# The start of an attention and FFN layer, its weight looks and its late flag on one Trainium2 core

## The chip, the core and the metric

The kernel runs on one core of a Trainium2 chip. The engines are TensorE (PE in the profile; PEld is its weight load), VectorE (DVE), ScalarE (ACT), GpSimd (POOL) and SyncE (SP, which only issues DMAs here). ACT and POOL also issue DMAs from their own queues; such rows carry a q (ACTq, SPq). The metric is the device time of one execution in microseconds (us), the median of several runs. A profile shows one execution.

## The reference

The inputs are x of 2 batches by 2048 rows by 256 features, four 256x256 attention weights, and a feed-forward net with 1024 hidden features whose weights hold only -1, 0 and 1, with a scale per output.

```
xn  = layernorm(x)
q, k, v = xn @ Wq, xn @ Wk, xn @ Wv
attn = softmax(causal(q @ k.T) / 16)          # one head of 256
a   = (attn @ v) @ Wo
h   = silu((xn @ w1.T) * s1) * ((xn @ w2.T) * s2)
h   = gelu((h @ h1.T) * sh1);  h = gelu((h @ h2.T) * sh2)     # exact gelu
out = x + a + (h @ w3.T) * s3
```

Everything is float32 and the outputs must be accurate to float32 inputs, so the kernel splits most operands into a high part that TensorE takes (fp32r) and a low part, the rest: a product is then two or three matmuls.

## The kernel before

**Stages.** The rows are cut into eight blocks of 512 (`TB`), four to a batch (`NB`). The attention of both batches comes first, then the feed-forward net. One branch lies between them: `ffn_ternary` for weights that are -1, 0 and 1, `ffn` for any others. The branch reads `flag`, which the attention stage works out while it runs.

**Start.** `load_x` fetches a block of x in two halves on SP. Wq and Wk come on ACT's queue. `weights_product` folds Wq and Wk into one matrix `wqk`, and later Wv and Wo into `wvo`; each half of a product has its own PSUM bank and copies (L260 to L267). `keys(n)` normalizes a block (`start_keys`: statistics L275 and L276 on VectorE, the root on ScalarE L280, four scalings on GpSimd L320), transposes it on TensorE (L346), and `hi_lo` (L251, L252) splits it on ScalarE and VectorE; the result also goes to DRAM (`xT_d`, L348) for the feed-forward stage. `queries` (L357), `score` (L401, mask L407, eviction with maximum L410) and `values` (L373) follow. Until x is there TensorE runs `WARM` matmuls on zeros (L247).

**Attention.** For each tile of 128 rows, `score` leaves its results in `s`, ScalarE takes the exponential (L422), and the tile is transposed: by blocks of 32 on VectorE (`turn_blocks`, L292) and two DMAs through DRAM (`d<-b` L297, `e<-d` L304), or for short tiles on TensorE (L465). Its high part pT is copied by ScalarE (L460, L251), the low part by GpSimd (L461) or VectorE, and `weigh` multiplies with the values (L479, L484; eviction L499 and L500). The second batch's x is normalized on GpSimd in the middle of this (L320), and its keys are split on ScalarE and GpSimd (L338, L339). Four PSUM banks `ps_0` to `ps_3` are used in turn by all products but `weigh` and the transposes.

**Looks.** Beside the attention the kernel looks through all feed-forward weights for a value that is not -1, 0 or 1. `items` lists the work and `beside(cost)` releases one step whenever enough matmul columns have gone by. `item_low` fetches a piece, rounds it on GpSimd (L134), masks the low bits on VectorE (L558) and adds them up on ScalarE (L560). `item_factors` takes two pieces of h1, forms four sums of their quarters on VectorE (`sum_up`, L153) into the buffer `xh0`, stores them (L581) and then runs `odd` on each piece: ScalarE takes the absolute value in place (L565), VectorE compares `(t != 0) != t` and adds up (L567). Its last step, `copy_factors`, copies three quarters of h1 from DRAM to DRAM on ACT's queue (L584, L586). `item_signs` runs `odd` on a piece of h2. The pieces arrive in two buffers `stg` by DMAs on ACT's queue (`fetched_weights`, L622); a fetch waits until the look that last used its buffer is done. `tc.issue_after(mark)` keeps an instruction behind a marked one of the main stream on its engine.

**The flag.** When the last look has been released, the loop at the end of the attention stage takes the maximum of all sums (L742), multiplies it into one number (L744) and copies it to `flag` (L745).

**Order.** Programs are written in stages, but the framework orders instructions per engine by a planned timeline when it builds the kernel; each engine then runs its list in order, and waits on semaphores. So a step may stand on its engine well before or after its place in the text.

**Feed-forward.** `ffn_ternary` runs on pairs of blocks: gated products (L172), then seven half-size products in place of eight for h1 and h2 (L850, with sums of weight quarters, the `factors`, read from DRAM), then w3 (L1011). The change does not touch it.

Of the kernel before, what the change touches and what calls it, by code (L numbers as in the profile page):

```python
# [31 lines left out]
TURN_KEYS = [8, 10, 12, 14]  # L32
LOOKS_FROM = 3
LEAD = 2
WARM = 14

STEPS = [("A11", "B11"), ("S1", "T1"), ("S2", "T2"), ("S4", "B22"), ("S3", "T3"), ("A12", "B21"), ("A22", "T4")]

SLOTS = {"h1": range(7), "h2": (0, 4, 1, 3, 2, 5, 6)}
LOW_BITS = 0xFFF


# [20 lines left out]
def attn_ffn_kernel(  # L65
# [57 lines left out]

    HB = H // 2
    HK = HC // 2
    factors = {k: dram.tile([P, len(STEPS), HK, HB], F32, name=f"factors_{k}") for k in ("h1", "h2")}


# [60 lines left out]
    with ExitStack() as actx:  # L189
# [19 lines left out]

        def bank():  # L210
            return in_turn("ps", ps_tiles)

        def load_x(n):
            t = xp.tile([P, NT, D], F32, tag="x", name=f"x_{n}")
            for h in range(2):
                src = x[n // NB, ds((n % NB) * TB + h * 2 * P, 2 * P), :]
                nc.sync.dma_start(out=t[:, ts(h, 2), :], in_=src.rearrange("(t p) d -> p t d", p=P))
            return t

        xs[NB - 1] = load_x(NB - 1)  # L220
        raw = {}
        for name, src in (("q", wqT), ("k", wkT)):
            raw[name] = stgp.tile([P, DC, D], F32, tag="stg", name=f"raw_{name}")
            nc.scalar.dma_start(out=raw[name], in_=src)
        nc.scalar.preload_act_table(AF.Sqrt)
        for n in range(NB - 2, -1, -1):
            xs[n] = load_x(n)

        ident = cp.tile([P, P], F32, name="ident")
        make_identity(nc, ident)  # L230
# [9 lines left out]
        nc.gpsimd.memset(ones, 1.0)  # L240


        idle = sp.tile([P, S], F32, tag="s", name="idle")[:, : TB // 2].bitcast(BF16)
        nc.vector.memset(idle, 0.0)
        ps_idle = bank()
        for _ in range(WARM):
            nc.tensor.matmul(out=ps_idle, lhsT=idle[:, :P], rhs=idle, start=True, stop=True)  # L247

        def hi_lo(hi, lo, src):

            nc.scalar.copy(hi, src)  # L251
            nc.vector.tensor_tensor(lo, src, hi.bitcast(F32), ALU.subtract)  # L252

        def weights_product(name, aT, b, factor):

            r = cp.tile([P, DC, 2, D], F32R, name=name)
            for c in range(DC):
                ps = bank()
                for d in range(DC):
                    nc.tensor.matmul(  # L260
                        out=ps[:, :D], lhsT=aT[:, d, ts(c, P)], rhs=b[:, d, :],
                        start=(d == 0), stop=(d == DC - 1),
                    )
                f = rp.tile([P, NT + 1, D], F32, tag="r", name=f"wf_{name}_{c}")[:, 0, :]
                nc.scalar.mul(f, ps[:, :D], factor)
                nc.vector.tensor_copy(r[:, c, 0, :], f)
                nc.vector.tensor_tensor(  # L267
                    r[:, c, 1, :], f, r[:, c, 0, :].bitcast(F32), ALU.subtract
                )
            return r  # L270

        def stats(xt, mv, n):
            for t in range(NT):
# [38 lines left out]
        def start_keys(n):  # L312
            xt = xs.pop(n)
            if n not in rstds:
                mv = cp.tile([P, NT, 2], F32, name=f"mv_{n}")
                stats(xt, mv, n)
                rstds[n] = root(mv, NT, str(n))
            rstd, off = rstds[n]
            for t in range(NT):
                nc.gpsimd.tensor_scalar(  # L320
                    xt[:, t, :], xt[:, t, :], rstd[:, t : t + 1], off[:, t : t + 1],
                    ALU.mult, ALU.add,
                )
            return xt
# [5 lines left out]
        def keys(n):  # L330
            ks[n] = kp.tile([P, DC, 2, TB], F32R, tag="k", name=f"k_{n}")
            if n in turned_keys:
                xT = turned_keys.pop(n).rearrange("p (t c) i q -> p c t i q", c=DC)
                for c in range(DC):
                    hi, lo = (
                        ks[n][:, c, a, :].rearrange("p (t i q) -> p t i q", t=NT, q=Q) for a in range(2)
                    )
                    nc.scalar.copy(hi, xT[:, c])  # L338
                    nc.gpsimd.tensor_tensor(lo, xT[:, c], hi.bitcast(F32), ALU.subtract)  # L339
# [8 lines left out]
            nc.sync.dma_start(out=xT_d[n], in_=ks[n].bitcast(F32).rearrange("p c h t -> p (c h t)"))  # L348

        def queries(n, m):  # L350
            if m == 0:
                qs[n] = in_turn("q", q_tiles)
            pp = bank()
            k = 0
            for c in range(DC):
                for a, b in ((0, 0), (0, 1), (1, 0)):
                    nc.tensor.matmul(  # L357
                        out=pp, lhsT=wqk[:, c, a, ts(m, P)], rhs=ks[n][:, c, b, :],
                        start=(k == 0), stop=(k == 3 * DC - 1),
                    )  # L360
                    k += 1
            hi_lo(qs[n][:, m, 0, :], qs[n][:, m, 1, :], pp)
# [18 lines left out]


        state, attn = {}, {}
        marks = {}

        def score(n, t, m, order):
            first = n - n % NB
# [8 lines left out]
            at = (m - first) * TB  # L396
            ps = bank()
            k = 0
            for c in range(DC):
                for a, b in ((0, 0), (0, 1), (1, 0)):  # L400
# [45 lines left out]
        def turn(n, t, m):  # L446
# [20 lines left out]
                )  # L467
            hi_lo(pT[:, 0, :w], pT[:, 1, :w], pt[:, :w])

        def weigh(n, t, m):  # L470
            first = n - n % NB
            st = state[n, t]
            if m == first:
# [87 lines left out]

        def odd(t):

            with tc.issue_after(marks["ACT"]):
                nc.scalar.activation(t, t, AF.Abs)  # L565
            with tc.issue_after(marks["DVE"]):
                nc.vector.scalar_tensor_tensor(  # L567
                    t, t, 0.0, t, ALU.not_equal, ALU.not_equal, accum_out=seen()
                )
# [24 lines left out]
        def item_factors(src, f, c):  # L594
# [12 lines left out]
        for src, dst in ((w1, w1_sb), (w2, w2_sb)):  # L607
            for c in range(src.shape[1]):
                item_low(src[:, c, :], dst[:, c, :])
# [92 lines left out]
        def before(j):  # L702
            if 3 <= j < 3 + NB:
                n = NB + j - 3
                x1 = xs[n] = load_x(n)
# [11 lines left out]
        now = 0  # L717
        until = -1
        j = -1
        checked = False  # L720
        while until < len(tiles) - 1:
            j += 1
            while until + 1 <= j - AHEAD:
# [12 lines left out]
            now += sum(cost for cost, _ in a + b)  # L736
            scored.append(now)
            merged(a, b, beside)
            if not looks and not checked:
                checked = True  # L740
                most = small.tile([P, 1], F32, tag="most", name="most")
                nc.vector.reduce_max(most, low_bits[:, : looked[0]], axis=AX.X)  # L742
                pf = bank()
                nc.tensor.matmul(out=pf[:1, :1], lhsT=most, rhs=ones, start=True, stop=True)  # L744
                nc.vector.tensor_copy(flag, pf[:1, :1])  # L745

        assert checked
# [474 lines left out]
```

## Time and profile before

| | before |
|---|---|
| median of 3 runs (lowest to highest) | 871.73 us (871.02 to 874.87) |
| the profiled execution's own time | 872.82 us |
| its span, first to last instruction | 871.1 us |
| busy TensorE, VectorE, ScalarE, GpSimd | 852.2, 620.4, 504.9, 296.4 us |
| feed-forward stage (from the branch on) | from about 287 us |
| TensorE's mean granted clock | 0.990 |

The span is cut into 40 slices in the page; a digit is a busy share in tenths, and PEclk is the clock that TensorE was granted, in tenths of full speed. In a timeline row the columns are start, length (of all the merged instructions), engine, line, operation, output and inputs, shape and count; in brackets stands how long the engine was idle before it and whom it waited for. In a row of the waits the numbers are the total, the count and the longest wait. A window row gives its length, then busy time and count for PE, PEld, DVE, ACT and POOL, then the granted clock, the busy share of the DMA engines and GB/s.

### The profile page before, as it was taken

What the parts mean: (1) busy time and instruction counts of PE and PEld (TensorE: products, weight loads), DVE (VectorE), ACT (ScalarE), POOL (GpSimd) and SP (SyncE); (2) the same over time, 40 slices, a digit from 0 to 9 for tenths busy, and PEclk for the clock granted to TensorE, in tenths of its full rate; (3) what the DMA queues carried; (4) which work ended last, traced back from release to release, by engine and by line L of the source; (5) the groups of instructions that cost most, each with busy time, mean ns of one, the idle gap of its engine ahead of it and who ended that gap; (6) DMA issues with size and microseconds to landing.
All of it is one profiled execution on the core that took longest, in us unless ns stands there. A gap on an engine that the chain in (4) does not pass through costs nothing.

```text
span 871.1 us, 12205 instructions
## 1 busy us (share of the span) xinstructions
PE 852.2 (98%) x4280; PEld 720.1 (83%) x4280; DVE 620.4 (71%) x1065; ACT 504.9 (58%) x881; POOL 296.4 (34%) x242
## 2 busy tenths in 40 slices
PE   8999799999999999999999999999999999999997
PEld 5988688888887878888988888988888898888887
DVE  5687664784764699996596596569468648848764
ACT  2556556764666456677256586536557635657670
POOL 4034857433544476550142050025024003502300
PEclk8999989999999999999999999999999999999999
DMA  9876499766792898854334434432444431144411
GB/s 307 331 250 212 152 348 292 265 214 194 251 343 62 340 400 309 312 192 146 111 109 150 144 144 146 148 121 103 146 145 145 146 136 58 50 144 145 145 49 53
DMA packets 62679, 162.53 MB, mean 187 GB/s; under 512 B 6544, under 2 KB 36368, under 8 KB 53264
## 3 DMA queue, kind: packets, MB, share of 16 engines
q1 hardware_dynamic: 56048, 141.73, 46.6%
q10 hardware_dynamic: 5472, 15.73, 5.3%
q0 software_dynamic: 1088, 4.19, 1.2%
q8 instruction: 36, 0.59, 0.3%
q14 instruction: 35, 0.29, 0.1%
HBM read 120.21 MB, written 47.71 MB: 193 GB/s over the span
## 4 chain that ended last, share of the span: by engine, by line
PE 75%; DMA 9%; DVE 6%; issue 3%; ACT 3%; POOL 2%; SPq 2%; ACTq 0%; POOLq 0%; DVEq 0%
PE ps_own L850 23%; PE ps L850 23%; PE ps L172 5%; PE ps_own L172 5%; PE ps L401 5%; DMA e<-d 4%; PE ps_own L1011 4%; PE ps L1011 4%; POOL pT L461 2%; DMA d<-b 2%; PE ps L373 2%; PE po L479 2%; PE ps L357 2%; SPq L304 1%; DMA d_x<-b 1%
## 5 line engine op out<-in xcount | busy, mean ns | idle before, releaser
L401 PE MATMUL ps<-k,q 128*128 128x512 f32 (+3 forms) x480 | 109.6, 366 | 0.0
L461 POOL TENSOR_TENSOR pT<-e,pT 128x512 fp32r<-128x512 f32 (+3 forms) x60 | 74.8, 1264 | 72.5 <-ACT pT L460 55.6
L401 PEld LDWEIGHTS ps<-k,q 128*128 128x128 f32 x480 | 82.0, 189 | 12.2
L479 PE MATMUL po<-v,pT 128*128 128x512 f32 x272 | 79.6, 406 | 6.6 <-ACT pT L460 6.5
L982 POOL TENSOR_TENSOR rt<-rt,xt 128x1024 f32<-128x1024 f32 x8 | 21.5, 2706 | 165.2 <-issue 114.7
L871 ACT ACTIVATE k_h_u<-k_h_u,h_s_sb 128x512 f32<-128x512 f32 x64 | 45.9, 722 | 38.1 <-DVE k_h_u L870 37.5
L830 POOL TENSOR_TENSOR k_h_u<-k_h_p,k_h_u 128x512 f32<-128x512 f32 x16 | 23.2, 1452 | 123.1 <-ACT q L185 106.3
L479 PEld LDWEIGHTS po<-v,pT 128*128 128x128 f32 x272 | 48.1, 193 | 14.5 <-ACT pT L460 7.2
L410 DVE TENSOR_SCALAR_CACHE_REDUCE s<-ps 128x512 f32<-128x512 f32 (+3 forms) x80 | 47.1, 600 | 12.1 <-PE ps L407 8.1
L422 ACT ACTIVATE s<-s,low 128x1024 f32<-128x1024 f32 (+7 forms) x48 | 43.0, 898 | 21.7 <-DVE low L416 21.7
L292 DVE STREAM_TRANSPOSE b<-s 128x1024 f32<-128x1024 f32 (+3 forms) x30 | 33.5, 1128 | 22.8 <-ACT s L422 20.5
L460 ACT CAST pT<-e 128x512 fp32r<-128x512 f32 (+3 forms) x60 | 32.4, 574 | 27.4 <-DMA e<-d 25.0
L484 PEld LDWEIGHTS po<-v,pT 128*128 128x128 f32 x272 | 42.0, 190 | 6.5 <-POOL pT L461 1.7
L484 PE MATMUL po<-v,pT 128*128 128x256 f32 x272 | 46.9, 286 | 0.2 <-POOL pT L461 0.2
L186 DVE TENSOR_TENSOR q<-k_h_u,q 128x512 fp32r<-128x512 f32 x32 | 45.9, 1462 | 0.0
L889 POOL TENSOR_TENSOR k_h_p<-f_h_B,k_h_p 128x512 f32<-128x512 f32 x16 | 34.4, 2175 | 21.2 <-DVE h_h_T L186 21.2
L500 POOL TENSOR_TENSOR r<-r 128x256 f32<-128x256 f32 x32 | 24.4, 765 | 49.7 <-ACT r L499 49.7
L830 POOL TENSOR_TENSOR f_w_B<-f_w_B,f_w_B 128x512 f32<-128x512 f32 x16 | 26.0, 1646 | 33.0 <-DVE f_w_B L181 33.0
L172 PE MATMUL ps<-xh,w_sb 128*128 128x512 f32 x144 | 35.9, 392 | 0.0
L870 DVE TENSOR_TENSOR k_h_u<-ps_own,k_h_u 128x512 f32<-128x512 f32 x32 | 21.7, 686 | 17.8 <-PE ps_own L850 17.8
L871 ACT ACTIVATE k_h_p<-k_h_p,h_s_sb 128x512 f32<-128x512 f32 x32 | 22.8, 722 | 18.6 <-DVE k_h_p L870 18.6
L850 PE MATMUL ps<-q,w_h_A 128*128 128x512 f32 x128 | 31.2, 393 | 1.5 <-DVE f_w_B L181 1.5
(176 smaller groups left out, 2201.3 us busy)
## 6 DMA issues: line engine op xcount, KB each, us to landing
w_h_S<-factors_h SPq DMA_DIRECT2D x32, 1024.0 KB, 4.7
w_h_A<-factors_h SPq DMA_DIRECT2D x24, 1024.0 KB, 4.7
d<-b SPq DMA_DIRECT2D x18, 512.0 KB, 3.5
e<-d SPq DMA_DIRECT2D x72, 128.0 KB, 3.6
xT_d<-k SPq DMA_DIRECT2D x8, 1024.0 KB, 7.3
stg<-in_ffn_h_w ACTq DMA_DIRECT2D x16, 512.0 KB, 5.6
x<-in_attn_x SPq DMA_DIRECT2D x16, 256.0 KB, 5.9
factors_h<-xh SPq DMA_DIRECT2D x4, 1024.0 KB, 4.8
```

What stands on the lines that cost most here:

```text
L172: nc.tensor.matmul(out=p, lhsT=w[:, c, ts(o, P)], rhs=xh[:, c, a, :], start=(c == 0 and a == 0), stop=(c == DC - 1 and a == 1),)
L186: nc.vector.tensor_tensor(r[:, 1, :], f, r[:, 0, :].bitcast(F32), ALU.subtract)
L401: nc.tensor.matmul(out=ps[:, :w], lhsT=qs[n][:, c, a, ts(t, P)], rhs=ks[m][:, c, b, :w], start=(k == 0), stop=(m < n and k == 3 * DC - 1),)
L410: marks["DVE"] = nc.vector.tensor_scalar(st["s"][:, ds(at, w)], ps[:, :w], 1.0, None, ALU.mult, ALU.max, accum_out=st["tops"][:, m - first ...
L422: marks["ACT"] = nc.scalar.activation(st["s"][:, at], st["s"][:, at], AF.Exp, bias=low, accum_out=st["sums"][:, u // UK : u // UK + 1],).ins
L461: nc.gpsimd.tensor_tensor(lo, src, hi.bitcast(F32), ALU.subtract)
L479: nc.tensor.matmul(out=st["po"], lhsT=pT[:, 0, ts(j, P)], rhs=vs[m][:, j, :, :], start=(m == first and j == 0), stop=False,)
L484: marks["PE"] = nc.tensor.matmul(out=st["po"][:, 0, :], lhsT=pT[:, 1, ts(j, P)], rhs=vs[m][:, j, 0, :], start=False, stop=(m == n and j == ...
L830: nc.gpsimd.tensor_tensor(B["B12"][i], B["B22"][i], B["B12"][i], ALU.subtract)
L850: nc.tensor.matmul(out=out[o], lhsT=w[:, c, ts(o, P)], rhs=sets[right][c][:, a, :], start=(start and c == 0 and a == 0), stop=(c == HK - 1 ...
L871: nc.scalar.activation(C[k][o], r[o] if r else banks[o], AF.Gelu, scale=s[:, at : at + 1])
L1011: nc.tensor.matmul(out=ys[t][:, :D], lhsT=h[c][:, a, ts(t, P)], rhs=w3_sb[:, c, :], start=(c == 0 and a == 0), stop=(c == HC - 1 and a == 1),)
```

## The change

The first block of x comes by SP and ACT's queue, one half each; Wq and Wv come behind it on SP, Wk and Wo on ACT's queue, with Wv and Wo in the buffer `b_1`. Both weight products are multiplied at the start, each into one bank, and copied in one piece later. Two of the four rows of the first xn are scaled by ScalarE. The statistics of the next blocks are kept behind `wqk`'s low part. The warm-up is 26 matmuls of half the width, with six more in the text behind the first keys. Queries and scores take the high parts first. h1's DRAM copies leave the looks and follow the four `xT_d` writes on SP. `odd` takes the absolute value by masking the sign bit on VectorE. The fetches of looked-at weights stay behind the last exponential. The flag is worked out in `judge`, called ahead of the last `weigh`.

```diff
-WARM = 14
+WARM = 26
+WARM_KEYS = 6
...
+MAGNITUDE = 0x7FFFFFFF
...
-        xs[NB - 1] = load_x(NB - 1)
-        raw = {}
-        for name, src in (("q", wqT), ("k", wkT)):
-            raw[name] = stgp.tile([P, DC, D], F32, tag="stg", name=f"raw_{name}")
-            nc.scalar.dma_start(out=raw[name], in_=src)
+        xs[NB - 1] = load_x(NB - 1, (nc.sync, nc.scalar))
+        raw = {name: stgp.tile([P, DC, D], F32, tag="stg", name=f"raw_{name}") for name in "qk"}
+        for i, name in enumerate("vo"):
+            raw[name] = b_tiles[1][:, i, :].rearrange("p (c d) -> p c d", c=DC)
+        for name, src, queue in (
+            ("q", wqT, nc.sync), ("k", wkT, nc.scalar), ("v", wvT, nc.sync), ("o", wo, nc.scalar)
+        ):
+            queue.dma_start(out=raw[name], in_=src)
...
+        def keep_warm(k):
+            for _ in range(k):
+                nc.tensor.matmul(
+                    out=ps_idle[:, : TB // 2], lhsT=idle[:, :P], rhs=idle[:, : TB // 2], start=True, stop=True
+                )
+
+        keep_warm(WARM)
...
             r = cp.tile([P, DC, 2, D], F32R, name=name)
+            ps = bank().rearrange("p (c d) -> p c d", c=DC)
             for c in range(DC):
-                ps = bank()
...
+            def copied():
+                f = rp.tile([P, NT + 1, D], F32, tag="r", name=f"wf_{name}")[:, :DC, :]
+                nc.scalar.mul(f, ps, factor)
+                nc.vector.tensor_copy(r[:, :, 0, :], f)
+                marks["lo"] = nc.vector.tensor_tensor(
+                    r[:, :, 1, :], f, r[:, :, 0, :].bitcast(F32), ALU.subtract
+                ).ins
+
+            return r, copied
...
+                with ExitStack() as behind:
+                    if n < NB - 1:
+                        behind.enter_context(tc.issue_after(first_lo))
+                    stats(xt, mv, n)
...
+                if n == NB - 1 and t % 2:
+                    nc.scalar.activation(
+                        xt[:, t, :], xt[:, t, :], AF.Identity,
+                        scale=rstd[:, t : t + 1], bias=off[:, t : t + 1],
+                    )
+                    continue
...
-            for c in range(DC):
-                for a, b in ((0, 0), (0, 1), (1, 0)):
+            for a, b in ((0, 0), (1, 0), (0, 1)):
+                for c in range(DC):
...
+        def judge():
+
+            assert not looks
+            most = small.tile([P, 1], F32, tag="most", name="most")
+            nc.vector.reduce_max(most, low_bits[:, : looked[0]], axis=AX.X)
+            with tc.issue_after(marks["PE"]):
+                pf = bank()
+                nc.tensor.matmul(out=pf[:1, :1], lhsT=most, rhs=ones, start=True, stop=True)
+            nc.vector.tensor_copy(flag, pf[:1, :1])
+
         def weigh(n, t, m):
+            if (n, t, m) == (N - 1, NT - 1, N - 1):
+                judge()
...
         def odd(t):
 
-            with tc.issue_after(marks["ACT"]):
-                nc.scalar.activation(t, t, AF.Abs)
             with tc.issue_after(marks["DVE"]):
+                nc.vector.tensor_scalar(t.bitcast(U32), t.bitcast(U32), MAGNITUDE, None, ALU.bitwise_and)
                 nc.vector.scalar_tensor_tensor(
...
         def copy_factors(src, f, c):
-            nc.scalar.dma_start(out=f[:, 0, c, :], in_=src[:, c, :HB])
-            for i in range(2):
-                nc.scalar.dma_start(out=f[:, 5 + i, c, :], in_=src[:, c + HK, ts(i, HB)])
+            with tc.issue_after(marks["SP"]):
+                nc.sync.dma_start(out=f[:, 0, c, :], in_=src[:, c, :HB])
+                for i in range(2):
+                    nc.sync.dma_start(out=f[:, 5 + i, c, :], in_=src[:, c + HK, ts(i, HB)])
...
-                (3000, lambda t: copy_factors(src, f, c)),
...
-                nc.scalar.dma_start(out=t, in_=src)
+                with tc.issue_after(marks["ACT"]):
+                    nc.scalar.dma_start(out=t, in_=src)
...
-        wqk = weights_product("wqk", raw["q"], raw["k"], scale)
-        for name, src in (("v", wvT), ("o", wo)):
-            raw[name] = stgp.tile([P, DC, D], F32, tag="stg", name=f"raw_{name}")
-            nc.scalar.dma_start(out=raw[name], in_=src)
+        wqk, wqk_copied = weights_product("wqk", raw["q"], raw["k"], scale)
+        wvo, wvo_copied = weights_product("wvo", raw["v"], raw["o"], 1.0)
         keys(NB - 1)
+        wqk_copied()
+        first_lo = marks["lo"]
+        keep_warm(WARM_KEYS)
         queries(NB - 1, 0)
         queries(NB - 1, 1)
         order = list(range(NB - 1, -1, -1))
         score(NB - 1, NT - 1, NB - 1, order)
-        wvo = weights_product("wvo", raw["v"], raw["o"], 1.0)
+        with tc.issue_after(marks["hi"]), tc.issue_after(marks["lo"]):
+            wvo_copied()
+        copy_factors(h1, factors["h1"], 0)
         for n in order[1:]:
             keys(n)
+            copy_factors(h1, factors["h1"], NB - 1 - n)
...
-            if not looks and not checked:
-                checked = True
-                most = small.tile([P, 1], F32, tag="most", name="most")
...
```

More of the change, by code (lines that the diff above doesn't have):

```diff
@@ L125, in attn_ffn_kernel @@
     HK = HC // 2
+    assert HK == 2 * DC == NB
     factors = {k: dram.tile([P, len(STEPS), HK, HB], F32, name=f"factors_{k}") for k in ("h1", "h2")}
@@ L211, in bank, with load_x @@
             return in_turn("ps", ps_tiles)
-        def load_x(n):
+        marks = {}
+        def load_x(n, queues):
             t = xp.tile([P, NT, D], F32, tag="x", name=f"x_{n}")
-            for h in range(2):
+            for h, queue in enumerate(queues):
                 src = x[n // NB, ds((n % NB) * TB + h * 2 * P, 2 * P), :]
-                nc.sync.dma_start(out=t[:, ts(h, 2), :], in_=src.rearrange("(t p) d -> p t d", p=P))
+                queue.dma_start(out=t[:, ts(h, 2), :], in_=src.rearrange("(t p) d -> p t d", p=P))
             return t
-        xs[NB - 1] = load_x(NB - 1)
-        raw = {}
-        for name, src in (("q", wqT), ("k", wkT)):
-            raw[name] = stgp.tile([P, DC, D], F32, tag="stg", name=f"raw_{name}")
-            nc.scalar.dma_start(out=raw[name], in_=src)
+        xs[NB - 1] = load_x(NB - 1, (nc.sync, nc.scalar))
[6 more added lines that the diff above has]
+            queue.dma_start(out=raw[name], in_=src)
         nc.scalar.preload_act_table(AF.Sqrt)
         for n in range(NB - 2, -1, -1):
-            xs[n] = load_x(n)
+            xs[n] = load_x(n, (nc.sync, nc.sync))
         ident = cp.tile([P, P], F32, name="ident")
@@ L240, in attn_ffn_kernel @@
         nc.gpsimd.memset(ones, 1.0)
-        idle = sp.tile([P, S], F32, tag="s", name="idle")[:, : TB // 2].bitcast(BF16)
+        idle = sp.tile([P, S], F32, tag="s", name="idle")[:, : TB // 4].bitcast(BF16)
         nc.vector.memset(idle, 0.0)
         ps_idle = bank()
-        for _ in range(WARM):
-            nc.tensor.matmul(out=ps_idle, lhsT=idle[:, :P], rhs=idle, start=True, stop=True)
+        def keep_warm(k):
[4 more added lines that the diff above has]
+        keep_warm(WARM)
         def hi_lo(hi, lo, src):
-            nc.scalar.copy(hi, src)
-            nc.vector.tensor_tensor(lo, src, hi.bitcast(F32), ALU.subtract)
+            marks["hi"] = nc.scalar.copy(hi, src).ins
+            marks["lo"] = nc.vector.tensor_tensor(lo, src, hi.bitcast(F32), ALU.subtract).ins
         def weights_product(name, aT, b, factor):
             r = cp.tile([P, DC, 2, D], F32R, name=name)
+            ps = bank().rearrange("p (c d) -> p c d", c=DC)
             for c in range(DC):
-                ps = bank()
                 for d in range(DC):
                     nc.tensor.matmul(
-                        out=ps[:, :D], lhsT=aT[:, d, ts(c, P)], rhs=b[:, d, :],
+                        out=ps[:, c, :], lhsT=aT[:, d, ts(c, P)], rhs=b[:, d, :],
                         start=(d == 0), stop=(d == DC - 1),
                     )
[L264 to L270, printed above, removed]
+            def copied():
[6 more added lines that the diff above has]
+            return r, copied
         def stats(xt, mv, n):
@@ L315, in start_keys @@
                 mv = cp.tile([P, NT, 2], F32, name=f"mv_{n}")
-                stats(xt, mv, n)
+                with ExitStack() as behind:
+                    if n < NB - 1:
+                        behind.enter_context(tc.issue_after(first_lo))
+                    stats(xt, mv, n)
                 rstds[n] = root(mv, NT, str(n))
@@ L347, in keys @@
                 hi_lo(ks[n][:, c, 0, :], ks[n][:, c, 1, :], pt)
-            nc.sync.dma_start(out=xT_d[n], in_=ks[n].bitcast(F32).rearrange("p c h t -> p (c h t)"))
+            marks["SP"] = nc.sync.dma_start(out=xT_d[n], in_=ks[n].bitcast(F32).rearrange("p c h t -> p (c h t)")).ins
         def queries(n, m):
@@ L383, in attn_ffn_kernel @@
         state, attn = {}, {}
-        marks = {}
         def score(n, t, m, order):
@@ L398, in score @@
             k = 0
-            for c in range(DC):
-                for a, b in ((0, 0), (0, 1), (1, 0)):
+            for a, b in ((0, 0), (0, 1), (1, 0)):
+                for c in range(DC):
                     nc.tensor.matmul(
@@ L605, in item_factors @@
             items.append(([src[:, c, :], src[:, c + HK, :]], steps))
-        for src, dst in ((w1, w1_sb), (w2, w2_sb)):
-            for c in range(src.shape[1]):
-                item_low(src[:, c, :], dst[:, c, :])
+        for c in range(HK):
+            src, dst = ((w1, w1_sb), (w2, w2_sb))[c // DC]
+            item_low(src[:, c % DC, :], dst[:, c % DC, :])
         w3_at = list(range(0, HC, SC // D))
@@ L704, in before @@
                 n = NB + j - 3
-                x1 = xs[n] = load_x(n)
+                x1 = xs[n] = load_x(n, (nc.sync, nc.sync))
                 with tc.issue_after(marks["DVE"]):
@@ L719, in attn_ffn_kernel @@
         j = -1
-        checked = False
         while until < len(tiles) - 1:
@@ L738, in attn_ffn_kernel @@
             merged(a, b, beside)
-            if not looks and not checked:
-                checked = True
-                most = small.tile([P, 1], F32, tag="most", name="most")
[L742 to L747, printed above, removed]
         last_quarter = [bank(), bank()]
```

## The prediction, made before the changed kernel ran

> **What bounds the kernel now.** I read the page's busy shares and slices first, then the waits of TensorE (PE), then windows and the timeline around the two places where PE is not both busy and at full clock.
>
> ```profile
> PE 852.2 (98%) x4280; PEld 720.1 (83%) x4280; DVE 620.4 (71%) x1065; ACT 504.9 (58%) x881; POOL 296.4 (34%) x242
> PE   8999799999999999999999999999999999999997
> PEclk8999989999999999999999999999999999999999
> ```
>
> PE is busy for 98% of the span, so 18.9 us is all the idle time there is, about 6.3 of it the tail after the last matmul, which the change does not touch. The fifth slice of PE (7) and the two slices with a clock of 8 are where something can be won.
>
> ```profile
> 8.00:11.00 3.00, 1.78 (x9) 0.80 (x8) 2.38 (x10) 1.00 (x3) 2.17 (x4) 0.99 1.08 387
> 11.00:17.00 6.00, 5.21 (x11) 3.64 (x12) 4.74 (x21) 1.40 (x5) 2.42 (x5) 0.50 0.89 287
> ```
>
> Windows: PE's busy time is the second number, the granted clock the one before the DMA share. From 8 to 11 us PE is busy for 1.78 of 3 us, and then the clock is 0.50 until 17. The first queries (L357) run there at half speed.
>
> ```profile
> PE po L479 <- ACT pT L460: 6.5, 4, 4.8
> PE ps L850 <- DVE f_w_B L181: 1.5, 2, 1.2
> PE ps L357 <- DVE v L252: 0.5, 1, 0.5
> ```
>
> Waits of PE: one single wait, 4.8 us for ScalarE's copy of pT, is a quarter of all PE idle time. The timeline shows its history:
>
> ```profile
> 102.14 4.38 DVE L153 TENSOR_TENSOR xh<-stg,stg 128x512 fp32r<-128x512 f32 x1
> 103.49 2.47 POOL L339 TENSOR_TENSOR k<-x,k 128x512 fp32r<-128x512 f32 x2
> 107.28 1.06 ACT L565 ACTIVATE stg<-stg 128x1024 f32<-128x1024 f32 x1 [3.80 <-DVE xh L153]
> 108.24 0.60 ACT L460 CAST pT<-e 128x512 fp32r<-128x512 f32 x1
> 108.36 1.23 DVE L567 SCALAR_TENSOR_TENSOR stg<-stg 128x1024 f32<-128x1024 f32 x1 [0.40 <-ACT stg L565]
> 108.89 2.08 PE L479 MATMUL po<-v,pT 128*128 128x512 f32 x4 [4.75 <-ACT pT L460]
> ...
> 110.68 1.18 DVE L567 SCALAR_TENSOR_TENSOR stg<-stg 128x1024 f32<-128x1024 f32 x1
> 111.79 0.68 DVE L410 TENSOR_SCALAR_CACHE_REDUCE s<-ps 128x512 f32<-128x512 f32 x1
> ...
> 113.45 2.96 PE L357 MATMUL ps<-k,wqk 128*128 128x512 f32 x12
> ```
>
> VectorE's (DVE's) sum L153, 0.69 in its other places, stands 4.38 beside GpSimd's (POOL's) run of two-input operations, which ends at 105.96. ScalarE (ACT) waits 3.80 for it with the look L565, and the pT copies stand behind that look. PE waits 4.75, and its clock falls:
>
> ```profile
> 104.00:109.00 5.00, 0.25 (x2) 0.11 (x1) 4.57 (x5) 1.72 (x3) 2.05 (x3) 0.75 0.09 35
> 109.00:114.00 5.00, 5.00 (x15) 3.86 (x16) 4.69 (x12) 2.47 (x5) 4.69 (x3) 0.56 1.02 321
> ```
>
> A mean clock of 0.56 over 5 us costs about 2.2 us more. So the place is worth about 7 us.
>
> **The start.** I work in the profiled run's time: span 871.1, its own time 872.8, which is 1.1 above the median of 871.7. In the order of the built kernel PE runs 32 warm-up matmuls of half the width, then the products of Wq Wk and of Wv Wo, then the first transposes, the queries, the first scores. The six extra warm-up matmuls meant for later stand in front with the rest. In the trace seven of the 14 old ones take 0.427 each, to 4.2 us, the others 0.22; so 32 halves end at 4.2 + 18 x 0.116 (a 128x256 of L484) = 6.3. The product took 1.97 for eight, so Wq Wk ends at 8.3 and Wv Wo at 10.2; eight transposes at 0.19 end at 11.8. Before, they ended at 10.73. So although xn is ready sooner (both halves of x at 4.4 where the second came at 6.02; two rows on POOL, 2 x 0.54, beside two on ACT, done at 8.3 and not 10.24), that gain is covered by the product moved in front. Four weight loads are 1 MB beside 0.5 MB of x; at the measured 370 to 400 GB/s they land by about 7, ahead of their use.
>
> From there: ACT's copies of k end at 12.6; eight queries need only k's high half and run to 14; DVE has four 0.36 statistics of the next x ahead of the first low half and three between the two, so the low halves come at 12.8 and 14.7, and the queries end at 15.3 (before 17.65). The next x is normalized by 18.2, q's low halves come at 18.7, the scores with their mask end at 19.1, the first values wait for wvo's low half until 20.35. Before, PE had reached the same count of matmuls at 22.47. Gain 2.1, if the clock stays at 1.00; bounds 0 (a second stretch at 0.50) and 4.4 (all of the queries' 2.35 and the product's 2.05).
>
> h1's twelve copies of 256 KB leave ACT's queue and stand on SP behind the four writes of xT, ahead of the first d<-b. By 40 us the queues have moved about 13 MB in both kernels, at up to 400 GB/s; the two early stg loads are gone from there, and I find the backlog done at 37 where d is issued at 40.5. Cost nothing; if it collides, the first pT has 1.3 us of slack at PE (ready 52.4, used 53.72), so at most 1.5. Hi-first order of queries and scores costs nothing in a stage where PE is busy throughout.
>
> **The looks.** Each of 16 `odd` loses 1.05 on ACT and gains an in-place bitwise_and on DVE:
>
> ```profile
> L558 DVE TENSOR_SCALAR stg<-stg x6: 687/1070/1759, 69.9 to 264.3; 128x1024 uint32<-128x1024 uint32 x6
> ```
>
> 0.69 with POOL quiet, 1.07 in the median, 1.76 beside POOL's L461. Now the place at 104, in before's time. The orders of DVE and POOL up to it are the same, so I expect the 4.38 again and the three sums done at 107.97. ACT no longer waits: pT comes at 104.8 and PE goes on after 0.9, then waits for POOL's low half (about 108), and comes to the queries at 109.4. These need a PSUM bank whose eviction (L410) stands on DVE behind two bitwise_ands, two L567 and a block transpose: 107.97 + 2 x 0.69 to 1.07 + 1.23 + 1.24 + 1.18 + 0.68 = 113.7 to 114.4. PE started L357 at 113.45. So the wait does not go, it changes its owner: from "ACT pT" to "DVE s". PE starts the queries 0.6 later, and cold after 4.6 us of idleness, where before it had warmed up by then; the price of that is the 2.2 above plus its first cold matmuls, I take 2.3. Together +2.9; bounds -4.0 (sum not blocked: below) and +5.4 (POOL's two L461, ready sooner now, go first and DVE loses 2.5 more). ACT's weight loads (L622) still wait on its queue for the look that frees their buffer, with pT copies behind them.
>
> The Trainium skill, in "SBUF — State Buffer", section "SBUF: two separate sides", says that DVE and GpSimd share one pair of ports as an exclusive lock, and that the loser is blocked for the whole instruction. By that rule every one of the 16 new operations can lose a POOL instruction of 1.27, which speaks against the change; the 1.76 of L558 agrees, its 0.69 elsewhere shows that it is not the usual price.
>
> Elsewhere PE's six waits between 120 and 280 make 2.75, 1.78 of it for ACT's pT, 0.80 for DVE. The first should shrink, the second grow by one pair of 0.69: I take 0, bounds -2.7 and +4.2 (three more pairs of looks, each 1.4 later).
>
> The flag: reduce_max, one small matmul (0.19) and the copy come before the last eight po matmuls; 1.4 us of these and 1.8 of gated products lie ahead of the flag's load on PE, which followed without a gap in the before trace. Cost 0; uncovered up to 1.5.
>
> The sum: -2.1 + 2.9 + 0 = +0.8, so 873.6 in the profiled run and 872.5 beside the median.
>
> The skill's page "TensorE: Matmul & The Clock Gate", section "What's actually happening", gives about 3.4 us of busy time to full clock; the trace has 3.0 at the start and 4.7 after 108.89. By the page the cold restart would cost 1.7 and the sum be 0.6 lower.
>
> **Rivals.** (1) The stall does go, faster. If the sum L153 meets no POOL run, it takes 0.69 and the evictions come at about 111.5: PE starts the queries 2 us sooner and never cools; with -2.1 at the start and -1.8 of ACT waits the time is 865.8. For: the other three L153 of that form took 0.69 to 0.81. Against: the same orders lead up to it. (2) DVE becomes the bound, slower. The pairs of looks near 160, 193 and 244 each hold the evictions 1.4 longer; PE has four score banks, some 5.4 us of work, and a pair with its transposes takes that. For: L357 waited 0.27 for L410 after the pair at 160. Against: DVE is busy for 65% there. 872.5 + 3 x 1.4 = 876.7, up to 879 with locks. (3) The start gives nothing: PE is busy only some 70% from 15.3 to 19, as it was before the clock fell at 11; then 872.5 + 2.1 = 874.6.
>
> **How the numbers follow.** No change 0.40 by the sum, rival 1 0.27, rival 2 0.26, rival 3 0.07. A difference of 0.5%, 4.4 us, is about what a measurement of this kernel can tell from no change. Faster is rival 1; same is the sum and rival 3; slower is rival 2. The likeliest case alone has 869 to 876; the range takes in rival 1 at its middle and most of rival 2: 864.5 to 878.
>
> **What would show it.** Right: no half clock between 11 and 17; about 2 us less at the first dense stretch; L565 gone from ACT; near 100 to 112 a wait "PE ps <- DVE s" of 4 to 5 us in place of "PE po <- ACT pT", and half clock after it. Wrong: PE without a wait over 2 us there (rival 1), or waits for DVE of over 1 us at 160, 193, 244 (rival 2); the flag's copy on the critical chain.

## The result and the profile after

| | before | after |
|---|---|---|
| median of 4 runs (lowest to highest) | 871.38 us (870.15 to 874.87) | 882.46 us (879.88 to 884.45) |
| the profiled execution's own time, its span | 872.82, 871.1 us | 881.87, 880.1 us |
| busy PE, DVE, ACT, POOL | 852.2, 620.4, 504.9, 296.4 us | 854.4, 637.1, 490.4, 299.7 us |

The ratio is 1.0122, 95% interval 1.0095 to 1.0149: slower by 1.2%, and 4.5 us above the range. The page of the changed kernel, the lines that answer to those shown of before:

```profile
PE 854.4 (97%) x4298; PEld 722.0 (82%) x4298; DVE 637.1 (72%) x1077; ACT 490.4 (56%) x865; POOL 299.7 (34%) x240
PE   9999789899999999999999999999999999999997
PEclk9999989999999999999999999999999999999999
```

ScalarE lost 14.5 us of work and VectorE gained 16.7, as the edit says. The 8 at the start of PEclk is gone; the 7 in PE's fifth slice has stayed, and its sixth and eighth slices are down to 8.

Waits of PE (total, count, longest):

```profile
PE po L516 <- ACT pT L485: 7.2, 7, 2.5
PE ps L383 <- DVE s L435: 5.5, 1, 5.5
PE po L521 <- POOL pT L486: 2.6, 6, 1.3
```

The one long wait has changed its owner, from ScalarE's pT to VectorE's eviction, as forecast, and is longer. Seven waits for ScalarE's pT, up to 2.5, and six for GpSimd's low part have come in beside it. The timeline of the place (before: 102 to 113 us):

```profile
99.74 6.84 DVE L156 TENSOR_TENSOR xh<-stg,stg 128x512 fp32r<-128x512 f32 x1
101.05 2.53 POOL L365 TENSOR_TENSOR k<-x,k 128x512 fp32r<-128x512 f32 x2
102.15 0.73 PE L516 MATMUL po<-v,pT 128*128 128x512 f32 x2 [1.13 <-ACT pT L485]
103.51 2.52 POOL L486 TENSOR_TENSOR pT<-e,pT 128x512 fp32r<-128x512 f32 x2
104.85 1.22 PE L521 MATMUL po<-v,pT 128*128 128x256 f32 x4 [1.32 <-POOL pT L486]
106.61 0.69 DVE L156 TENSOR_TENSOR xh<-xh,stg 128x512 fp32r<-128x512 f32 x1
107.95 1.29 DVE L602 TENSOR_SCALAR stg<-stg 128x1024 uint32<-128x1024 uint32 x2
109.15 1.22 DVE L603 SCALAR_TENSOR_TENSOR stg<-stg 128x1024 f32<-128x1024 f32 x1
...
112.57 0.69 DVE L435 TENSOR_SCALAR_CACHE_REDUCE s<-ps 128x512 f32<-128x512 f32 x1
113.32 2.93 PE L383 MATMUL ps<-k,wqk 128*128 128x512 f32 x6 [5.54 <-DVE s L435]
```

The sum L156 starts 2.4 us earlier than its like before (L153 at 102.14) and ends at 106.58, where it ended before (106.52): it lasts 6.84 and not 4.38. GpSimd's run now goes on through two L486 to 106.03, because ScalarE no longer waits with a look and hands over pT at once. Everything behind the sum on VectorE is late by that, and TensorE stands still three times, 7.99 us together (4.75 before), with the clock falling twice:

```profile
104.00:109.00 5.00, 2.93 (x8) 2.02 (x8) 4.97 (x6) 0.00 (x0) 2.03 (x2) 0.66 0.01 2
109.00:114.00 5.00, 0.68 (x2) 0.59 (x3) 5.00 (x11) 1.18 (x2) 1.13 (x1) 0.75 0.95 270
```

VectorE (third of the busy times) is full for the ten microseconds, TensorE (first) works for 3.6 of them. In the clock's records of the two traces TensorE was at 0.50 before from 106.5 to 113.4, working for 4.46 of it; after from 104.7 to 108.1 and from 111.5 to 118.4, working for 7.98. At half speed the half of that is lost: 2.2 before, 4.0 after.

To place the rest I matched the two traces by work done: for a given sum of matmul work (each line by its usual duration, warm-up and flag left out), the lag is how much later this kernel's PE reaches it than before's. Averaged over 75 to 90 us of before's time it is -3.7, over 117 to 128 it is +2.2, over 600 to 700 +9.3. So: **start -3.7, place near 104 +5.9, behind it +7.1**; my terms were -2.1, +2.9 and 0. Behind the place TensorE's clock stays up (1.00 from 118.4 to 876 us); what grows there are the waits for ScalarE's pT, from 1.8 us before to 5.0 between 120 and 280 us.

### The profile page after: what moved, and what is told of

It reads as the page before. It is cut to its first block, busy times and chain, and to the rows that moved or that the text cites. A ratio compares the mean times of both kernels' runs of the same rounds, so it can differ in the third digit from the quotient of the medians.

```text
span 880.1 us, 12224 instructions
## 1 busy us (share of the span) xinstructions
PE 854.4 (97%) x4298; PEld 722.0 (82%) x4298; DVE 637.1 (72%) x1077; ACT 490.4 (56%) x865; POOL 299.7 (34%) x240
## 4 chain that ended last, share of the span: by engine, by line
PE 79%; DMA 7%; DVE 7%; ACT 2%; issue 2%; SPq 1%; POOL 1%; ACTq 0%; POOLq 0%; DVEq 0%
PE ps_own L882 23%; PE ps L882 22%; PE ps L175 7%; PE ps_own L175 6%; PE ps L426 6%; PE ps_own L1043 3%; PE ps L1043 3%; DMA d<-b 3%; PE po L516 3%; PE ps L399 2%; DVE xh L156 2%; DMA e<-d 1%; PE po L521 1%; DVE b L309 1%; SPq L321 1%
## 5 line engine op out<-in xcount | busy, mean ns | idle before, releaser
L486 POOL TENSOR_TENSOR pT<-e,pT 128x512 fp32r<-128x512 f32 (+3 forms) x60 | 76.0, 1286 | 70.8 <-ACT pT L485 55.3
L537 POOL TENSOR_TENSOR r<-r 128x256 f32<-128x256 f32 x32 | 27.5, 860 | 56.5 <-ACT r L536 56.5
L536 ACT ACTIVATE r<-po,inv 128x512 f32<-128x512 f32 x32 | 22.0, 687 | 23.5 <-PE po L521 22.0
```

The lines of the kernel that those rows point to most:

```text
L486: nc.gpsimd.tensor_tensor(lo, src, hi.bitcast(F32), ALU.subtract)
```

## The experiments

All are edits of the changed kernel unless they say "before". Each was compared with runs of the kernel before on its own chip. "Start", "place" and "behind" are the three steps of the lag just defined, from each kernel's profile. A profile is one execution, and it can lie up to 3.9 us from the kernel's median (e15 and e7 3.9 and 3.7 above, e12 2.6 below). If the total is taken from the ratio instead, single entries of "behind" move by up to 4 us (e15 to -1.7, e12 to +3.8, e17 to +4.1), so a difference of 2 or 3 us in that column tells nothing.

| kernel | median us | ratio to before (95%) | start | place | behind |
|---|---|---|---|---|---|
| changed kernel | 882.46 | 1.0122 (1.0095 to 1.0149) | -3.7 | +5.9 | +7.1 |
| e1 looks on ScalarE | 875.05 | 1.0046 (1.0029 to 1.0062) | -3.6 | -0.5 | +5.8 |
| e2 before, looks on VectorE | 875.11 | 1.0036 (1.0021 to 1.0051) | -0.3 | +4.2 | -0.6 |
| e3 sums on GpSimd | 867.76 | 0.9954 (0.9935 to 0.9973) | -3.2 | -4.1 | +3.8 |
| e4 start and flag alone | 872.37 | 1.0007 (0.9990 to 1.0023) | +1.4 | -1.7 | -1.5 |
| e5 free fetches | 886.45 | 1.0157 (1.0133 to 1.0181) | +1.6 | +4.8 | +8.5 |
| e6 before, sums on GpSimd | 876.36 | 1.0049 (1.0032 to 1.0066) | +0.2 | -4.6 | +9.9 |
| e7 e3 and free fetches | 875.06 | 1.0047 (1.0027 to 1.0068) | +1.3 | -5.1 | +10.4 |
| e8 e3 and looks on ScalarE | 868.61 | 0.9961 (0.9943 to 0.9980) | -3.6 | -2.8 | +3.3 |
| e9 empty step | 876.97 | 1.0057 (1.0034 to 1.0080) | -4.0 | +6.0 | +3.1 |
| e10 e1 and empty step | 880.03 | 1.0074 (1.0048 to 1.0100) | -2.7 | +2.3 | +9.2 |
| e11 e3 and empty step | 867.07 | 0.9934 (0.9913 to 0.9955) | -4.4 | -3.0 | +4.4 |
| e12 first four sums on GpSimd | 869.88 | 0.9972 (0.9952 to 0.9991) | -4.1 | -2.1 | +0.9 |
| e13 early flag | 882.10 | 1.0107 (1.0081 to 1.0134) | -3.7 | +5.9 | +8.7 |
| e14 two lows on VectorE | 878.30 | 1.0073 (1.0049 to 1.0097) | -3.6 | +4.5 | +4.9 |
| e15 e12 and looks on ScalarE | 866.64 | 0.9926 (0.9900 to 0.9952) | -2.6 | -2.1 | +2.3 |
| e16 e12 and empty step | 868.13 | 0.9948 (0.9927 to 0.9969) | -4.0 | -2.9 | +2.2 |
| e17 copies back | 881.88 | 1.0132 (1.0101 to 1.0163) | -0.8 | +8.2 | +1.0 |
| e18 e12 and copies back | 875.04 | 1.0051 (1.0034 to 1.0068) | +1.4 | -1.9 | +3.6 |

**Which part cost it: the looks (e1, e2), the start (e4).** e1:

```diff
 def odd(t):
+    with tc.issue_after(marks["ACT"]):
+        nc.scalar.activation(t, t, AF.Abs)
     with tc.issue_after(marks["DVE"]):
-        nc.vector.tensor_scalar(t.bitcast(U32), t.bitcast(U32), MAGNITUDE, None, ALU.bitwise_and)
```

e2 is the reverse edit in the kernel before. e4 is e1 with two more parts undone (the edits of e5 and e17): the bond of the fetches, which is the `tc.issue_after` line that keeps them behind the last exponential, and the copies' place behind the `xT_d` writes on SP.

> The changed kernel with one part undone: odd takes the absolute value on ScalarE again. Theory A, the looks on VectorE cost everything that was lost: with the look back on ScalarE the pT copies stand behind it again, GpSimd's run near 100 us ends sooner, the sum L156 takes 4.4 and not 6.84, and the start's 3.3 us stay; 871.4 - 3.3 = 868, between 866 and 870. Rival B, the other moves (fetches kept behind the last exponential, h1's copies on SP, the late flag) lost the 4 to 7 us that went after 120 us: 872 to 876, with PE waits for ACT pT near 148 and 160 as in the changed kernel.

> The kernel before with one part of the change alone: odd masks the sign bit on VectorE in place of the absolute value on ScalarE. Theory A: the sum near 102 us is blocked for 6.8 and not 4.4, TensorE waits there for VectorE's eviction, and 5 to 7 more us go after 120 us: 871.4 + 12.5 = 884, between 880 and 886. Rival B: only the 5 us of the place near 102 are lost, 874 to 878. A third reading, that the loss needs the earlier start, gives 871 to 874.

> The changed kernel with the looks on ScalarE, h1's copies in the looks on ACT's queue and the fetches without their bond to the last exponential: only the start and the late flag are left of the change. Theory A: as with the look alone undone, 868 (866 to 870), the two within 1.5 us of each other. Rival B, the copies on SP and the bound fetches cost 4 to 7: this kernel 868, the one with the look alone undone 872 to 876. My prediction's own term for the start alone was -2.1: 869.3.

Theory A, that the looks cost everything, fell: e1 takes 875, not 868, and e2 875, not 884. By the ratios the moved look costs 3.1 us alone (e2) and 6.6 on top of the other parts (e1 to the changed kernel). In e2 the sum is blocked for 7.1, the place costs 4.2 and nothing is lost behind it:

```profile
101.44 7.12 DVE L154 TENSOR_TENSOR xh<-stg,stg 128x512 fp32r<-128x512 f32 x1
105.49 2.52 POOL L462 TENSOR_TENSOR pT<-e,pT 128x512 fp32r<-128x512 f32 x2
115.30 2.07 PE L358 MATMUL ps<-k,wqk 128*128 128x512 f32 x4 [6.82 <-DVE s L411]
```

The +4.2 lies within my bounds for the place (+2.9, at most +5.4), though with a sum of 7.1 and not the 4.38 that I had put there, and in the kernel before my 0 for the rest was right. e4, where I expected 868 from either theory, gained nothing: its start is 1.4 later, not 3.7 earlier. So two parts that I had costed at nothing carry the start's gain; e5 and e17 below.

**What held the sum (e3, e12, e14).** e3 is one word; e12, in which the number c of the piece is passed in, does the same for the first piece of h1 alone:

```diff
 def sum_up(tiles, i):
     with tc.issue_after(marks["DVE"]):
-        sums_of_factors(sums, tiles, (i,), nc.vector)
+        sums_of_factors(sums, tiles, (i,), nc.gpsimd)   # e12: nc.vector if c else nc.gpsimd
```

e14 leaves the sums and takes two operations out of GpSimd's run:

```diff
-    nc.gpsimd.tensor_tensor(lo, src, hi.bitcast(F32), ALU.subtract)
+    engine = nc.vector if (n, t) == (2, 3) and m < 2 else nc.gpsimd
+    engine.tensor_tensor(lo, src, hi.bitcast(F32), ALU.subtract)
```

> The changed kernel with the sums of h1's quarters (sum_up, L156) on GpSimd and not on VectorE. Theory A, the sum's 6.84 us are VectorE's wait for GpSimd's run of two-input operations, which ends only when that run ends: no VectorE operation takes over 2.5 us near 100, TensorE has no wait of over 2 us for VectorE's s there, its clock stays up, and 5 to 9 us come back in spite of 16 more operations of about 1.3 us on GpSimd: 873 to 878. If the sum was slow of itself (its own inputs or output, not the neighbour), GpSimd's sums take the same 5 to 7 us and hold the pT low parts: 882 or more.

> The changed kernel with the four sums of the first piece of h1 alone on GpSimd, the other twelve on VectorE as they were. If the place near 100 us is the cause of all, the later loss included, this is as good as all sums on GpSimd: 867 to 869. If the later loss comes from the later sums on VectorE (each held 0.5 to 0.9 by GpSimd) and from the looks, the lead is 7 us at 120 and 1 or 2 at the end: 871 to 875.

> The changed kernel with two of GpSimd's operations taken out of its run near 100 us: the low parts of pT of the two tiles that joined the run (row tile 3 of the third block, first two key blocks) are formed on VectorE. If the sum lasts until GpSimd's run ends, it now ends 0.55 us after the two L365, 4.3 us long and not 6.84. VectorE has two more operations of 0.69 ahead of its evictions, so TensorE's wait for s becomes only some 1 us shorter; the time 876 to 882. If the sum keeps 6.8, its length has another cause than the run.

e3 is the sharpest result: 14.7 us less than the changed kernel, more than the 5 to 9 that I expected, and faster than before. e12 moves four operations and takes 12.6 off. Its place:

```profile
100.65 1.28 POOL L156 TENSOR_TENSOR xh<-stg,stg 128x512 fp32r<-128x512 f32 x1
101.87 2.53 POOL L365 TENSOR_TENSOR k<-x,k 128x512 fp32r<-128x512 f32 x2
104.22 4.46 PE L383 MATMUL ps<-k,wqk 128*128 128x512 f32 x12 [1.19 <-DVE s L435]
104.33 2.55 POOL L486 TENSOR_TENSOR pT<-e,pT 128x512 fp32r<-128x512 f32 x2
```

On GpSimd the sum takes 1.28 and holds nobody for long; PE's queries start at 104.22 and not 113.32, after a wait of 1.19 and not 5.54. e14 shows that the length of the sum at this place is the rest of the run:

```profile
99.60 4.39 DVE L156 TENSOR_TENSOR xh<-stg,stg 128x512 fp32r<-128x512 f32 x1
100.94 2.51 POOL L365 TENSOR_TENSOR k<-x,k 128x512 fp32r<-128x512 f32 x2
```

With the two L486 gone the run ends at 103.45 and the sum at 103.99. In five kernels with sums of 4.38 (before), 4.73 (e1), 4.39 (e14), 6.84 (after) and 7.12 us (e2) the sum ends 0.54 to 0.56 after GpSimd's last operation, and so it does in e5, e9, e10 and e13 (7.23, 6.58, 4.40 and 7.25): there it gets its turn at no boundary inside the run, and then takes some 0.55.

That is a fact of this place and not a rule. Later in the changed kernel's own trace a sum of the same form meets a run of GpSimd, and has its turn as soon as the one operation in progress ends:

```profile
144.30 2.52 POOL L365 TENSOR_TENSOR k<-x,k 128x512 fp32r<-128x512 f32 x2 [1.63 <-ACT k L364]
145.88 1.49 DVE L156 TENSOR_TENSOR xh<-stg,stg 128x512 fp32r<-128x512 f32 x1
146.78 1.18 POOL L537 TENSOR_TENSOR r<-r 128x256 f32<-128x256 f32 x1
```

L365 ends at 146.82 and the sum at 147.37, and the next operation, L537, takes 1.18 where its median is 0.74. The other fifteen sums of the changed kernel take 0.68 to 1.63. In e4 and e17 the very sum of this place takes 1.12 and 1.53. So what decides between one operation and the whole run I have not shown.

e14's time, 878.3, is in the range expected, though the wait is another: TensorE now waits 3.60 and 1.61 us for the two low parts, which stand behind the sum in VectorE's list, and there no longer for s.

**Does it hold when other parts are changed (e8, e9, e10, e11, e15, e16)?** e8 and e15 put the look back on ScalarE beside the sums on GpSimd. The empty step keeps the looks' former pace, from which the change took a step:

```diff
     (3000, lambda t: odd(t[1])),
+    (3000, lambda t: None),
```

> The changed kernel with the sums on GpSimd and the absolute value back on ScalarE. It tells what the moved look is worth once no sum holds VectorE. By the change's own purpose, ScalarE's looks hold pT copies and it is slower than the 867.8 of sums on GpSimd with looks on VectorE: 869 to 872. By my theory that the moved look only lengthens VectorE's list, and is itself held by GpSimd's runs, 864 to 867.

> The changed kernel with an empty step where h1's copies stood in the looks, so that the looks keep the pace that they had before (3000 matmul columns, about 1.25 us, later behind each of four pieces). All kernels without that step lost 4 to 10 us after 120 us, the three with it 0 or less. Theory E, the looks' new pace puts them beside the late pT and evictions: the loss after 120 us goes from 7 to about 1, 875 to 877; the place near 100 is the same. Rival F, the pace is nothing and the later loss follows from the stall and the looks on VectorE: 881 to 884.

> The changed kernel with the look on ScalarE and the empty step: the start, the copies on SP, the bound fetches and the late flag are left of the change. Theory E: the start's 3.3 us and the 4.3 us of lead after the place near 100 are kept: 867 to 869. Rival F: as with the look alone undone, 873.5 to 876.5.

> The changed kernel with the sums on GpSimd and the empty step. Theory E: the 7.2 us of lead after the place near 100 are kept but for 1 or 2: 865 to 866.5. Rival F: 867 to 869, as without the step.

> The changed kernel with the first four sums on GpSimd and the look on ScalarE. If the first sums are the whole cause and where the look stands then matters no more, 868 to 871, as with looks on VectorE (869.9). If looks on ScalarE hold pT copies, 872 or more.

> The changed kernel with the first four sums on GpSimd and the empty step in the looks. If the later loss is a consequence of the stall at 100, it does not come back when the looks' pace is shifted: 868 to 871. If it is a matter of where the looks fall, whatever happened at 100, the time can be 4 to 8 us off: 864 to 866 or 874 to 878.

All six kernels with the first sums on GpSimd and the start as changed (e3, e8, e11, e12, e15, e16) take 866.6 to 869.9; the six with that start and all sums on VectorE (the changed kernel, e1, e9, e10, e13, e14) take 875.1 to 882.5. Pair by pair, moving the first four sums is worth 12.6 (e12), 8.4 (e15 against e1), 8.8 (e16 against e9) and 6.8 us (e18 against e17); by the ratios, which take out the chip, 13, 10, 9 and 7. Once they are away, the look's engine matters little: e3 and e8 take 867.8 and 868.6; of e12 and e15, 869.9 and 866.6, the one with the look on ScalarE is ahead. Neither forecast for e8 came out. Theory E, the pace of the looks, was right for e9 (877) and refuted by e10 (880 and not 868): by the ratios the same empty step makes the changed kernel 5.7 faster, and e1 no faster (2.4 slower, with intervals that overlap).

**Parts costed at nothing (e5, e7, e13, e17, e18).** e5 and e7 take the line `with tc.issue_after(marks["ACT"])` from `fetched_weights`. e17 and e18 put `copy_factors` back on `nc.scalar` and into the looks. e13 calls `judge()` when the list of looks is empty, as before.

> The changed kernel with the fetches of looked-at weights free of their bond to the last exponential, all else as changed. In the three profiles with the bond TensorE is idle for 6 to 9 us between 120 and 345 us, in the three without it for 3 to 4. Theory C, the bond shifts the fetches into the blocks' transfers and makes the pT late: idle time after 120 falls to about 4 and the time to 877 to 879, the stall for the blocked sum near 100 stays. Rival D, the blocked sums and the looks on VectorE alone make those waits: no change, 881 to 884.

> The changed kernel with the sums on GpSimd and the fetches free of their bond. Theory C: 4 us less than with the sums on GpSimd alone (867.8), so 863 to 865. Rival D: the same, 866.5 to 869. If the bond protects the first blocks of x from early weight transfers, the start is 1 to 3 us later and the time is 869 to 871.

> The changed kernel with the flag worked out as soon as the last look is released, as before. My prediction put the late flag at 0, bounded by 1.5. Right: 881 to 884, as the changed kernel. If the late flag or what it holds back costs something: 1 to 3 us less.

> The changed kernel with h1's copies back on ACT's queue and as a step of the looks; the bound fetches, the looks on VectorE and all else stay. Theory G, the copies behind the keys cause the loss after 120 us (it was 0 or less in the three kernels with copies on ACT's queue and sums on VectorE): the loss of 7.1 falls to 1 or less, while the start loses 2 to 5 us to twelve early issues on ACT's queue: 877 to 881, with the place near 100 us as in the changed kernel. Rival F, the loss after 120 follows no single part: 4 us or more remain there, 883 to 887.

> The same with the first four sums on GpSimd. The start's loss of 2 to 5 us by the copies on ACT's queue is the only difference from the kernel with the first sums on GpSimd (869.9): 872 to 875. If the copies' place does nothing at the start, 868 to 871.

Theory C fell: without the bond the time is 4 to 7 us longer, outside every range that I had put up for e5 and e7. In e5 the fetches go out at 10.29, and GpSimd's rounding of the fetched weights (L137) comes to stand ahead of its scaling of the second x, and waits for the fetch; TensorE waits for x:

```profile
18.68 1.09 POOL L137 TENSOR_SCALAR w_sb<-stg 128x1024 fp32r<-128x1024 f32 x1 [3.64 <-DMA stg<-in_ffn_w_w]
19.77 2.58 POOL L346 TENSOR_SCALAR x<-x,rstd,off 128x256 f32<-128x256 f32 x4
20.80 1.23 PE L372 MATMUL ptx<-ident,x 128*128 128x128 f32 x4 [3.00 <-POOL x L346]
```

The scaling starts at 15.44 in the changed kernel. By the start column the bond is worth 5.3 (e5) or 4.5 us (e7 against e3), the copies' place 2.9 (e17) or 5.5 (e18 against e12). The flag costs nothing that these runs can tell (882.1). Theory G was right on the start and not shown for the rest: e17's column has 1.0 behind the place, but its place grew to 8.2 and its ratio, 1.0132, is no better than the changed kernel's; e18 loses 3.6.

**Sums on GpSimd in the kernel before (e6).**

> The kernel before with one thing changed: the sums L153 on GpSimd. Theory A: no VectorE operation is held for over 2.5 us near 104, the look and the pT copies behind it come early, the 4.75 us wait and the 2.2 us of half clock are gone, 16 GpSimd operations of 1.3 us each come in beside: 864 to 868. If the place is worth nothing because the next wait is as late, 870 to 872.

The place gave its 4.6, as theory A says, and 9.9 were lost behind it, so 876.4, above both ranges. There the look on ScalarE follows a sum that now comes late on GpSimd, with pT copies behind it; that this is the cause of all 9.9 I have not shown.

**What stays open.** The loss behind the place lies between -1.5 and +10.4 over these kernels, and no single edit switches it. It is a few waits at other places in each kernel. In the changed kernel the largest is:

```profile
158.08 1.14 ACT L364 CAST k<-x 128x512 fp32r<-128x512 f32 x2 [5.58 <-DMA x<-d_x]
159.60 0.82 ACT L485 CAST pT<-e 128x512 fp32r<-128x512 f32 x2
160.27 1.21 PE L516 MATMUL po<-v,pT 128*128 128x512 f32 x4 [2.46 <-ACT pT L485]
```

ScalarE waits with the next keys for a transfer, and pT stands behind them in its list. In e1 a pT is 3.18 late at 196.6, in e18 3.24 at 131.1, in e7 3.88 at 262.2; in e10 TensorE waits 2.29 for VectorE's s at 197.5, in e9 2.21 for its q at 154.8. With the first sums on GpSimd (e12, e15, e16) the loss is 0.9 to 2.3, and with the stall 3.1 to 8.7 in the changed kernel, e9, e13 and e14. But it is -0.6 and 1.0 in e2 and e17, which lose 4.2 and 8.2 at the place, and e1, e6 and e7 lose 5.8, 9.9 and 10.4 behind it without losing there. So by these columns the stall is neither needed nor enough for it. That it is how the transfers happen to fall is a guess, and no run settles it.

**The best version** is faster than both kernels: e15, 866.64 us, ratio 0.9926, and e11, 867.07, ratio 0.9934, which their intervals don't tell apart. Both keep the changed start and move sums to GpSimd.

## Why the prediction was wrong

Two steps failed: the term for the place near 104, whose sum on VectorE I took to last as long as before, and the term for the rest of the attention, which I put at 0. The cause of the first is shown, that of the second, the larger one, stays open. The sum of my steps was +0.8; in the lag it is -3.7 + 5.9 + 7.1 = +9.3.

- **The start: right in kind, too small.** -3.7 against -2.1. There is no half clock from 11 to 17, and the first scores' mask (L432) stands at 18.18 where I had 19.1. Two terms were mis-sized: the eight transposes took 1.04 (0.13 each) and not 1.52, and wvo's low half was done at 18.77, not 20.35.
- **The place: the right mechanism, mis-sized, and with the answer in the text.** The owner of the wait changed as forecast. The term that failed is "the 4.38 again". I argued that the orders of the two engines are the same; but the sum's length is set by when GpSimd's run ends, and that is a matter of time, not of order. In the same paragraph I had pT come at 104.8, 3.4 earlier, and did not carry it to GpSimd's run, which eats pT; I kept it as the upper bound: "ready sooner now, go first and DVE loses 2.5 more", +5.4. The runs show 2.46 more and +5.9. Nor is a sum "0.69 in its other places": in the trace of before, others of them take up to 1.31 beside GpSimd, held by one operation, and that difference was there to be asked about. Of the 5.9, 3.2 is more idle time and 1.8 more half clock; 0.9 I can't name.
- **Elsewhere: 0 against +7.1, outside its bounds of -2.7 to +4.2.** I took the bounds from before's small waits. The waits for ACT's pT were to shrink; they grew from 1.8 to 5.0. That is the larger part of the miss. Over the kernels the loss runs from -1.5 to +10.4; e2, e4, e12 and e17 alone stay within 1.5 of my 0.
- **The flag: 0, right as far as e13 can tell. Copies and fetches: I looked only for what they cost, and both are what lets the start gain** 2.9 to 5.5 and 4.5 to 5.3; a part that only protects another has its price in that part's cover.
- **Rivals.** Rival 1 is what e12 shows for the place when the sum meets no wait: queries 9 us sooner than in the changed kernel, no long wait, though the clock still falls for 3.4 us. Its 865.8 is near the 866.6 to 869.9 of those kernels, but with other terms: they gain more at the start and lose again behind the place. Rival 2 had the right sign by the wrong mechanism: behind 120 us TensorE waits for pT, not for the pairs of looks at 160, 193 and 244. Rival 3 is wrong.
- **The rules weighed.** By the Trainium skill, "SBUF — State Buffer", section "SBUF: two separate sides", the loser of the shared ports is blocked for a whole instruction. Most sums here agree, the 1.49 above for one. The 6.84 shows more: six GpSimd operations behind the one that the sum met, with no turn for VectorE between them. For the new operations the price that I feared did not come:

```profile
L602 DVE TENSOR_SCALAR stg<-stg x16: 676/690/1778, 108.0 to 262.1; 128x1024 uint32<-128x1024 uint32 x16
```

The median of the sixteen is 0.69; the shared resource hurt an operation that was there all the time. The skill's page "TensorE: Matmul & The Clock Gate", section "What's actually happening", has a free-running window of about 3.4 us: the spells of 0.50 in the attention stage are 3.4, 6.8 and (e14) 10.2 long, whole multiples of it. The 4.7 after 108.89 in my prediction is 4.5 by the clock's records.

## What to carry to other kernels

A VectorE operation with two inputs in SBUF that stands beside a run of GpSimd can last until the run ends. Here it did so at one place in nine kernels (4.4 to 7.3 us), and the other fifteen sums of the changed kernel waited for one operation at most (up to 1.63 in all): price it both ways, and ask of each edit whether it lengthens the run. Freeing an engine also speeds what feeds on it; follow the freed data to its next reader before taking a duration over from the old trace. Where a tuned pipeline has long chains of transfers, give the term "elsewhere" the width that re-ordering alone shows, here -1.5 to +10.4 us, and not the size of the old waits.

## What was not expected of the hardware

Near 100 us VectorE got no turn at any boundary between GpSimd's instructions in nine kernels, for up to 7.25 us for an operation of 0.69, and in every case until 0.54 to 0.56 before its own end. Elsewhere in the same traces it got one at the first boundary. A masking operation with one SBUF input is held too: in e3 one L602 took 3.57 beside GpSimd's L486, L156 and L537, and ended 0.55 after the last of them. In the same run VectorE's subtraction with one input in PSUM (L266) took its usual 0.69 beside the L486:

```profile
110.54 0.69 DVE L266 TENSOR_TENSOR q<-ps,q 128x512 fp32r<-128x512 f32 x1
111.14 3.57 DVE L602 TENSOR_SCALAR stg<-stg 128x1024 uint32<-128x1024 uint32 x1
```

The clock fell at 104.7 us in the changed kernel although TensorE had worked for 1.37 of the 3.41 us before, with two gaps of 1.13 and 1.32 and none longer; in e12 it fell at 104.0 after 1.40 of 3.41.
